# A four-layer graph network on one core: norm roots, ReLU, block kinds and planner costs of the first stage, and new planner costs elsewhere

## The chip, the cores and the metric

The kernel runs on one core of a Trainium2 chip, as one launch. Its time is the device time in microseconds of one execution. "Before" is the kernel as it stands, and the profile shown is of one execution of it.

A core has five engines that work at once, each through its own queue in strict order: TensorE (PE in the profile; its weight loads are PEld), VectorE (DVE), ScalarE (ACT), GpSimd (POOL), and SyncE (SP), which here only issues DMAs.

## The reference, cut to what matters

There are 128 graphs of 128 nodes with 128 channels: `x` is [128, 128, 128] in fp32, `adj` is [128, 128, 128] of 0 and 1. Four layers follow each other; each normalises its input, takes the ReLU, and adds its result to `x`.

```python
h = jnp.maximum(_layernorm(x, axis=-1), 0.0)
x = x + _L0_gnn_ref(h, adj, ...)     # layers 1, 2, 3: attention of other kinds
```

The first layer is what the first stage of the kernel works for:

```python
D = jnp.abs(x[:, :, None, :] - x[:, None, :, :])     # |h_i - h_j| of all pairs of nodes
h = jnp.einsum('bijc,oc->bijo', D, W1) + b1          # 64 outputs
m = jnp.mean(h, axis=(0, 1, 2))
v = jnp.mean((h - m) ** 2, axis=(0, 1, 2))
h = (h - m) / jnp.sqrt(v + EPS) * g1 + be1
```

The mean and variance run over all graphs and all pairs, so they have to be known before any pair's score can be used. The rest of the first layer (scores on the edges, softmax, a product with the nodes, a second batch norm over all graphs), and then layers 1 to 3, need them.

## The kernel before

Three stages follow each other.

`statistics()` computes only the mean and variance of the pair values. It works on groups of 4 graphs (`GB`), 32 groups in all. `nodes(g)` loads a group's `x`, normalises it (mean and variance on VectorE; the root, `(var + eps) ** -0.5`, by an add and a pow on GpSimd; subtraction and multiplication on GpSimd), transposes it on TensorE into PSUM (`pt`), and lets ScalarE take the ReLU twice: into SBUF (`he`) and in place in PSUM (`pt`). It also splits the 64 products of each node into three bf16 parts (`us`). `block(b, q)` then treats 32 rows of one graph against 64 (or 63) later nodes each; 4 blocks cover half of all pairs, which is enough because the difference is symmetric. A block is:

- a difference of `he` with its own nodes, 128 x 2048 or 2016 values, on VectorE (all `q == 0`, and 3 or 4 of the 4 blocks `q == 1` of a group) or on GpSimd (the rest, 8 or 9 of 16),
- the absolute value on ScalarE, in place,
- 4 products with `w1T` on TensorE, two of them side by side in the array, into `ph` (3 buffers of two PSUM banks),
- the statistics of `ph`: by two `bn_stats` on VectorE, or by a Square with accumulated sums on ScalarE (the blocks in `by_act`).

Some blocks `q == 0` (the set `larger`) use |a - b| = 2 max(a, b) - a - b: VectorE takes the maximum instead of the difference, ScalarE does nothing, and TensorE adds 12 bf16 products of `both` with the three parts of `us`.

`edge_attention()` computes the first layer's scores, attention and second batch norm. `layers_01()` does what is left for groups of 4 graphs, with up to 8 groups under way.

In every stage the steps are Python generators. Before each step a generator says `yield engine, cost, takes, frees`: the engine, the microseconds that the step is assumed to keep it, and the buffers that it takes and gives back. `in_order` simulates the engines with these costs, always lets the step begin that can begin first, and emits the instructions in that order; `AFTER` adds 0.2 us (2.2 us for a DMA) from the end of a step until its result counts as usable. So the costs set the order of every engine's queue, and with it that of the loads and stores on SP's queue, but nothing else: on the chip each instruction waits for its data.

```python
free_at[engine] = now + work
end = now + work + AFTER[engine]
```

Of the kernel before, what the change touches and what calls it, by code (L numbers as in the profile page):

```python
# [14 lines left out]
AF = mybir.ActivationFunctionType  # L15
ALU = mybir.AluOpType
# [10 lines left out]
GB = 4  # L27
# [29 lines left out]
PE, ACT, DVE, POOL, DMA = "PE", "ACT", "DVE", "POOL", "DMA"  # L57
# [115 lines left out]
def kernel(ctx: ExitStack, tc: tile.TileContext, x, adj, w, out):  # L173
# [316 lines left out]
    def statistics():  # L490

        with tc.tile_pool(name="a2", bufs=2) as a2, tc.tile_pool(
# [6 lines left out]
            larger = {(i, 0) for i in range(3)}  # L501
            by_act = {(i, 3) for i in range(GB)} | {(1, 2), (3, 2)}
# [17 lines left out]
            def nodes(g):  # L520
# [5 lines left out]
                yield DVE, 1.3, "", ""  # L526
# [6 lines left out]
                yield POOL, 3.3, "xn", "xg"  # L533
                rs = a2.tile([P, GB], F32, tag="ln_rs", name="ln_rs")
                nc.gpsimd.tensor_tensor(rs, mv[:, :, 1], eps, ALU.add)
                nc.gpsimd.tensor_tensor(rs, rs, nhalf, ALU.pow)
# [4 lines left out]
                yield PE, 0.45, "pt", "xn"  # L541
# [3 lines left out]
                yield ACT, 1.0, "he", ""  # L545
# [3 lines left out]
                nc.scalar.activation(pt, pt, AF.Relu)  # L549
# [4 lines left out]
                yield PE, 0.8, "ph us", ""  # L554
# [4 lines left out]
                yield ACT, 0.31, "", ""  # L559
                nc.scalar.copy(us[:, 0], pu)  # L560
                yield DVE, 0.36, "", ""
                nc.vector.tensor_tensor(pu, pu, us[:, 0], ALU.subtract)
                yield ACT, 0.31, "", ""
                nc.scalar.copy(us[:, 1], pu)
                yield DVE, 0.34, "", "ph"
# [4 lines left out]
            def pairs(b):  # L570
# [10 lines left out]
                if not left[g]:  # L581
                    yield "free", "he pt us"
                    yield DVE, 0.5, "", "six"
                    nc.vector.bn_aggr(st[:, g, :], six.pop(g).rearrange("p a b -> p (a b)"))

            def block(b, q):
# [7 lines left out]
                is_larger, on_act = (i, q) in larger, (i, q) in by_act  # L594
                by_dve = q == 0 or (q == 1 and (i < 3 or g % 2))
                yield "after", ("six", g)
                yield (DVE, 2.26, "d", "") if by_dve else (POOL, 3.58, "d", "")
# [5 lines left out]
                if by_dve:  # L603
                    own = bcast(hp[:, i0 : i0 + QR], 2, w_)
                    nc.vector.tensor_tensor(dv, later, own, ALU.max if is_larger else ALU.subtract)  # L605
# [4 lines left out]
                if not is_larger:  # L610
                    yield ACT, 2.1 if on_act else 1.92, "", ""
# [4 lines left out]
                yield PE, 3.15 if is_larger else 1.73, "ph", "d"  # L616
# [16 lines left out]
                if on_act:  # L633
                    yield ACT, 1.25, "", "ph"
# [3 lines left out]
                else:  # L638
                    yield DVE, 1.42, "", "ph"
# [60 lines left out]
    def edge_attention():  # L700
# [3 lines left out]
        with tc.tile_pool(name="b2", bufs=2) as b2p, tc.tile_pool(name="b3", bufs=B_W) as b3p, tc.tile_pool(  # L704
# [80 lines left out]
            def group(g):  # L785
# [12 lines left out]
                yield POOL, 0.85, "", ""  # L798
# [7 lines left out]
                yield POOL, 1.9, "", ""  # L806
# [3 lines left out]
                yield PE, 0.85, "p p", ""  # L810
# [5 lines left out]
                yield DVE, 0.8, "", "p"  # L816
# [7 lines left out]
                yield DVE, 1.9, "", "p"  # L824
# [6 lines left out]
                yield PE, 0.4, "p", ""  # L831
# [30 lines left out]
            def parts(g, xn, made):  # L862
                yield ACT, 0.6, "", ""
                h1 = tile_h("h1")
                nc.scalar.activation(h1, xn, AF.Relu)
                yield DVE, 0.62, "", ""
# [4 lines left out]
                yield POOL, 1.8, "", ""  # L871
# [5 lines left out]
            def values(g, ht, made):  # L877
                yield PE, 1.0, "p", ""
# [3 lines left out]
                yield ACT, 0.6, "", "p"  # L882
# [3 lines left out]
            def check(g, adjb):  # L886

                yield PE, 0.6, "p", ""
# [6 lines left out]
                yield ACT, 0.75, "", "p"  # L895
# [7 lines left out]
            def bases(g, adjb, made):  # L903
                yield ACT, 0.6, "", ""
                base = tile_f("base")
                nc.scalar.activation(base, adjb, AF.Identity, bias=far, scale=-NEG)
                yield POOL, 1.9, "", ""
# [5 lines left out]
            def graph(g, i, inc, made):  # L913
# [3 lines left out]
                yield PE, 0.95, "q", ""  # L917
# [8 lines left out]
                yield ACT, 0.75, "d", "q"  # L926
                d = b2p.tile([P, 2, SLOT_N // 2], F32, tag="d", name="d", bufs=3)
                nc.scalar.activation(d, diff[:, :, 0 : SLOT_N // 2], AF.Abs)  # L928
                yield PE, 0.6, "p", "d"
# [3 lines left out]
                yield ACT, 0.5, "", "p"  # L933
                z = made["z"][:, i, :]
                nc.scalar.activation(z, ph, AF.Identity, bias=h_bi, scale=h_sc)  # L935
                yield DVE, 0.48, "", ""
                leaky(nc.vector, z, z, 0.01)
                yield PE, 0.5, "p", ""
# [11 lines left out]
                yield DVE, 0.13, "", "p"  # L950
# [10 lines left out]
                yield ACT, 0.75, "it", ""  # L961
                it = b2p.tile([P, 5, P], F32, tag="it", name="it", bufs=3)
                nc.scalar.copy(it, pi)  # L963
                yield DVE, 0.75, "", "p"
# [4 lines left out]
                yield PE, 1.25, "" if i else "p", "it"  # L969
# [8 lines left out]
            def attention(g, made):  # L978
                yield DVE, 1.45, "", "p"
# [6 lines left out]
                yield ACT, 2.1, "", ""  # L986
# [7 lines left out]
                yield DVE, 0.8, "", ""  # L994
# [3 lines left out]
                yield PE, 0.5, "p", ""  # L998
# [3 lines left out]
                yield ACT, 0.6, "eT", "p"  # L1002
                eT = tile_f("eT", 2)
                nc.scalar.copy(eT, pt)
                yield PE, 1.0, "p", ""
# [9 lines left out]
                yield DVE, 1.5, "", "w yt"  # L1015
# [501 lines left out]
    def layers_01(first_in):  # L1517

        with tc.tile_pool(name="c_in", bufs=3) as c_in, tc.tile_pool(
# [31 lines left out]
            def normal(x, out):  # L1551

                yield DVE, 1.75, "", ""
# [6 lines left out]
                yield ACT, 0.45, "", ""  # L1560
# [3 lines left out]
                yield POOL, 2.5, "t", ""  # L1564
# [5 lines left out]
            def transposed(xn, out, frees):  # L1570
                yield PE, 1.1, "ps", frees
# [3 lines left out]
                yield ACT, 0.62, "t", "ps"  # L1575
# [8 lines left out]
            def single_head(z, own, mask, least, values, ones_at, after, out):  # L1584

                yield ACT, 1.6 if own else 0.7, "t", "ps"
# [8 lines left out]
                yield DVE, 0.72, "", ""  # L1595
                masked_larger(t.rearrange(flat), mask.rearrange(flat), least)
                yield "join",
                yield PE, 1.1, "pz", "t v"
                po = weighted(t, values, ones_at + 1)
                yield DVE, 0.9, "t", "pz"  # L1600
                xh = over_sums(po, ones_at)
                yield "fork", positive(xh, after, out)
                yield ACT, 0.65, "t", ""
# [3 lines left out]
                yield DVE, 0.7, "", "t t t"  # L1607
# [5 lines left out]
            def positive(xh, after, out):  # L1613
                yield DVE, 0.62, "t", ""
# [34 lines left out]
            def with_bias3(x3):  # L1649
                yield POOL, 0.95, "", ""  # L1650
                nc.gpsimd.tensor_tensor(x3, x3, bcast(pb_bc, 1, GC), ALU.add)

            def head_attention(i, f1d, fl, mask, es, ps_):
                yield PE, 0.45, "pz w", ""
# [7 lines left out]
                yield ACT, 1.27, "", ""  # L1662
# [5 lines left out]
                yield DVE, 1.27, "", "pz"  # L1668
# [3 lines left out]
            def two_graphs(k, f1d, fl, mask, h1T, es, xT):  # L1672
# [4 lines left out]
                yield PE, 1.0, "ps vals", ""  # L1677
# [3 lines left out]
                yield DVE, 0.7, "", "ps"  # L1681
# [5 lines left out]
                yield PE, 2.6, "ps ps", "w w vals"  # L1687
# [18 lines left out]
                yield ACT, 1.25, "t", "ps"  # L1706
# [4 lines left out]
                yield DVE, 0.69, "", "ps t"  # L1711
# [4 lines left out]
            def type_scores(t, h3T, dstT, by_type):  # L1716
                yield PE, 0.63, "ps", ""
                pp = psum("pp")
                nc.tensor.matmul(pp, aq[:, t, :], h3T, start=True, stop=True)  # L1719
                yield ACT, 0.6, "t", "ps"  # L1720
# [4 lines left out]
            def with_h1(xn, x1, res):  # L1725
                yield DVE, 0.69, "t", "t t"
# [701 lines left out]
```

## Time and profile before

| what | value |
|---|---|
| median of 3 runs | 2766.36 us (2764.8 to 2766.55) |
| the profiled execution | 2765.68 us, span 2763.8 us |
| mean granted TensorE clock | 0.970 |
| busy share of the span | PE 92%, DVE 86%, ACT 78%, POOL 61% |
| first stage | 28 to about 1133 us |
| second stage | about 1133 to 1830 us |
| third stage | about 1830 to 2764 us |

The busy shares of the whole span mix three stages with different limits. They have to be read stretch by stretch: which engine is full, and who waits for whom. A row of a group of instructions names the line, the engine, the operation and its tiles, then the count, the busy time, the mean duration of one, and how long the engine had stood idle before such instructions and what ended that.

### The profile page before, as it was taken

To read this page: it belongs to the slowest core of one execution; us is meant where nothing else is said; L and a number is where in the kernel's file an instruction comes from. 1 tells how busy PE (TensorE), PEld (TensorE's weight loads), DVE (VectorE), ACT (ScalarE), POOL (GpSimd) and SP (SyncE) were. 2 spreads that over 40 slices of the span, in tenths; PEclk is the share of its full clock that TensorE was granted. 3 is DMA by queue.
4 is the path that set the end of the run, shared out by engine and by line. 5 is a ranking of instruction groups with operands and counts; after the bars stand their busy time and mean duration, and the time that the engine had idled before them with its cause. 6 is when DMAs were issued, how large, how long until landed. Compare 5 with 4: busy or idle time off the path is not lost. (4 is left out here: it accounts for less than half of the span.)

```text
span 2763.8 us, 52563 instructions
## 1 busy us (share of the span) xinstructions
PE 2529.2 (92%) x19981; PEld 1568.7 (57%) x19981; DVE 2376.3 (86%) x4596; ACT 2148.8 (78%) x3563; POOL 1675.7 (61%) x1007
## 2 busy tenths in 40 slices
PE   6999999999999999799999999967989988988887
PEld 2334343343434343377777777756767766777665
DVE  6999999899999998778888888859889887888986
ACT  4999999999999999656666666548788887788885
POOL 7999999999999999644443434112333333333225
PEclk8999999999999999899999999979999999999999
DMA  2000000000000000322222222030111110111001
GB/s 67 17 31 24 24 24 24 24 24 24 23 24 24 24 20 12 121 82 89 79 92 75 83 83 77 19 126 21 44 36 45 47 57 28 45 43 32 9 5 29
DMA packets 134261, 122.67 MB, mean 44 GB/s; under 512 B 9504, under 2 KB 100960, under 8 KB 134000
## 3 DMA queue, kind: packets, MB, share of 16 engines
q1 hardware_dynamic: 131360, 117.83, 13.8%
q8 instruction: 161, 2.64, 0.4%
q10 hardware_dynamic: 2032, 1.31, 0.2%
q14 instruction: 100, 0.82, 0.1%
q0 software_dynamic: 608, 0.07, 0.0%
HBM read 73.05 MB, written 46.14 MB: 43 GB/s over the span
## 5 line engine op out<-in xcount | busy, mean ns | idle before, releaser
L608 POOL TENSOR_TENSOR d<-he 128x2016 f32<-128x2016 f32 (+1 forms) x272 | 959.5, 3561 | 12.1 <-PE ph L629 12.1
L629 PE MATMUL ph<-d,w1T 128*64 128x512 f32 (+1 forms) x4096 | 911.3, 594 | 23.4 <-ACT d L612 16.2
L612 ACT ACTIVATE d<-d 128x2016 f32<-128x2016 f32 (+1 forms) x416 | 772.6, 1885 | 5.2 <-POOL d L608 4.1
L629 PEld LDWEIGHTS ph<-d,w1T 128*64 128x64 f32 x4096 | 314.9, 136 | 538.5 <-issue 454.5
L605 DVE TENSOR_TENSOR d<-he,pt 128x2048 f32<-128x2048 f32 x240 | 542.2, 2274 | 6.9 <-PE ph L629 6.2
L641 DVE BATCH_NORM_STATS2 six<-ph 128x6 f32<-128x512 f32 (+1 forms) x640 | 405.0, 681 | 64.9 <-PE ph L629 63.9
L1566 POOL TENSOR_TENSOR xn<-xo,mv 128x512 f32<-128x512 f32 x64 | 77.7, 1214 | 311.6 <-DVE mv L1559 222.0
L635 ACT ACTIVATE ph<-ph 128x1008 f32<-128x1008 f32 x192 | 191.5, 998 | 51.2 <-PE ph L629 35.3
L973 PE MATMUL pl<-its,it 128*128 128x128 f32 x1280 | 171.6, 283 | 7.0 <-DVE its L966 6.7
L873 POOL CAST h<-xn 128x512 bf16<-128x512 f32 x32 | 20.0, 626 | 253.7 <-DVE xn L867 201.1
L973 PEld LDWEIGHTS pl<-its,it 128*128 128x128 f32 x1280 | 157.0, 195 | 21.7 <-DVE its L966 13.4
L1669 DVE SCALAR_TENSOR_TENSOR p<-z,mask 128x1024 f32<-128x1024 f32 x124 | 148.5, 1212 | 11.7 <-ACT z L1667 11.6
L1567 POOL TENSOR_TENSOR xn<-xn,rs 128x512 f32<-128x512 f32 x96 | 108.1, 1126 | 67.1 <-ACT rs L1563 55.9
L629 PE MATMUL ph<-both,us 128*64 128x512 bf16 x1152 | 142.3, 380 | 0.0
L935 ACT ACTIVATE z<-ph,h_bi,h_sc 128x320 f32<-128x320 f32 x128 | 78.4, 619 | 77.2 <-PE ph L932 76.6
L1667 ACT ACTIVATE z<-z 128x1024 f32<-128x1024 f32 x128 | 129.0, 1008 | 4.1
L921 PE MATMUL diff<-inc,h 128*128 128x320 bf16 x768 | 129.2, 305 | 0.7 <-ACT d L928 0.5
L841 DVE SCALAR_TENSOR_TENSOR inc<-in_row,row 128x12 bf16<-128x12 f32 (+12 forms) x512 | 125.7, 314 | 3.7 <-PE in_row L834 3.6
L928 ACT ACTIVATE d<-diff 128x640 f32<-128x640 f32 x128 | 89.9, 702 | 49.1 <-PE diff L921 48.6
L963 ACT CAST it<-pi 128x640 f32<-128x640 bf16 x128 | 86.6, 689 | 50.7 <-PE pi L960 50.2
L629 PEld LDWEIGHTS <-us 128*64 128x64 bf16 x1152 | 73.4, 111 | 90.7 <-issue 56.9
L1914 POOL TENSOR_TENSOR xh<-xh,xo 128x512 f32<-128x512 f32 x32 | 45.5, 1422 | 124.7 <-DVE xh L1635 108.7
(350 smaller groups left out, 5422.4 us busy)
## 6 DMA issues: line engine op xcount, KB each, us to landing
ht<-h SPq DMA_DIRECT2D x64, 256.0 KB, 2.8
xg<-in_x SPq DMA_DIRECT2D x32, 256.0 KB, 2.8
n<-ln_xn SPq DMA_DIRECT2D x32, 256.0 KB, 2.4
h<-he SPq DMA_DIRECT2D x32, 256.0 KB, 2.6
adj<-in_adj SPq DMA_DIRECT2D x32, 256.0 KB, 3.2
xn<-n SPq DMA_DIRECT2D x32, 256.0 KB, 2.7
xb<-in_x SPq DMA_DIRECT2D x32, 256.0 KB, 3.2
xb<-xb SPq DMA_DIRECT2D x32, 256.0 KB, 2.0
```

The costliest lines, as they stand in the source:

```text
L605: nc.vector.tensor_tensor(dv, later, own, ALU.max if is_larger else ALU.subtract)
L608: nc.gpsimd.tensor_tensor(dv, later, own, ALU.subtract)
L612: nc.scalar.activation(d[:, 0 : 4 * n], d[:, 0 : 4 * n], AF.Abs, accum_out=sums[:, g, k : k + 1] if on_act else None,)
L629: nc.tensor.matmul(ph[64 * a : 64 * a + 64, t, 0:n], wt, x_, start=part == 0, stop=not is_larger or part == 3,)
L635: nc.scalar.activation(ph[:, :, 0:n], ph[:, :, 0:n], AF.Square, accum_out=squares[:, g, k : k + 1])
L641: nc.vector.bn_stats(six[g][:, 2 * by_bn.index((i, q)) + t, :], ph[:, t, 0:n])
L841: nc.vector.scalar_tensor_tensor(inc[:, :, e : e + n], in_row[:, :, 0:n], float(k + 1), row[:, :, 0:n], ALU.is_equal, ALU.subtract,)
L921: nc.tensor.matmul(diff[:, a, 0 : SLOT_N // 2], h[:, i, :], inc[:, a * SLOT_N // 2 : (a + 1) * SLOT_N // 2], start=m == 0, stop=m == 2,)
L973: nc.tensor.matmul(made["pl"][:, i, :], it[:, k, :], its[:, k, :], start=k == 0, stop=k == 4)
L1567: nc.gpsimd.tensor_tensor(xn, xn, bcast(rs, 2, P), ALU.mult)
L1667: nc.scalar.activation(z, z, AF.Exp, scale=1.0 - SLOPE)
L1669: nc.vector.scalar_tensor_tensor(p, z, 1.0, bcast(mask[:, i, :], 1, NH), ALU.max, ALU.mult)
```

## The change

In the first stage:

- The roots of the norm go from GpSimd (add and pow) to ScalarE (Ln, then Exp with scale -0.5, on 128 x 4 values). The activation table that has both is loaded at the head of the stage.
- ScalarE no longer writes the ReLU back into `pt`. VectorE's differences read the unrectified `pt` and rectify it on the way: `tensor_tensor(later, own)` becomes `scalar_tensor_tensor(max(own, 0), later)`.
- Two blocks of a group use the maximum (`i < 2`) where three did.
- One block of a group, (3, 2), has its statistics on VectorE instead of ScalarE: 11 and 5 where 10 and 6 were.

In all three stages the costs in the `yield` lines are replaced. Outside `statistics()` nothing else changes.

```diff
@@ -491,6 +491,7 @@
+        nc.scalar.preload_act_table_set("natural_log_exp_and_others")
         with tc.tile_pool(name="a2", bufs=2) as a2, tc.tile_pool(
             name="a_d", bufs=A_D
         ) as a_d, tc.tile_pool(name="a_ph", bufs=3, space=PSUM) as a_ph, tc.tile_pool(
@@ -498,8 +499,7 @@
         ) as a_ps:
             n_parts = NB // GB
             blocks = [(i, q) for i in range(GB) for q in range(NQ)]
-            larger = {(i, 0) for i in range(3)}
-            by_act = {(i, 3) for i in range(GB)} | {(1, 2), (3, 2)}
+            by_act = {(i, 3) for i in range(GB)} | {(1, 2)}
             by_bn = [k for k in blocks if k not in by_act]
             ACT_N, BN_N = (
                 sum(QR * width[q] for _, q in some) for some in (sorted(by_act), by_bn)
@@ -523,46 +523,46 @@
                 yield DMA, 0.6, "xg", ""
                 xg = a2.tile([P, GB, P], F32, tag="xg", name="xg")
                 nc.sync.dma_start(xg, x_t[:, b0 : b0 + GB, :])
-                yield DVE, 1.3, "", ""
+                yield DVE, 1.6, "", ""
                 s6 = a2.tile([P, GB, 6], F32, tag="ln_s6", name="ln_s6")
                 mv = a2.tile([P, GB, 2], F32, tag="ln_mv", name="ln_mv")
                 for i in range(GB):
                     nc.vector.bn_stats(s6[:, i, :], xg[:, i, :])
                     nc.vector.bn_aggr(mv[:, i, :], s6[:, i, :])
-                yield POOL, 3.3, "xn", "xg"
+                yield ACT, 0.35, "", ""
                 rs = a2.tile([P, GB], F32, tag="ln_rs", name="ln_rs")
-                nc.gpsimd.tensor_tensor(rs, mv[:, :, 1], eps, ALU.add)
-                nc.gpsimd.tensor_tensor(rs, rs, nhalf, ALU.pow)
+                nc.scalar.activation(rs, mv[:, :, 1], AF.Ln, bias=eps_c)
+                nc.scalar.activation(rs, rs, AF.Exp, scale=-0.5)
+                yield POOL, 2.1, "xn", "xg"
                 xn = a2.tile([P, GB, P], F32, tag="ln_xn", name="ln_xn")
                 nc.gpsimd.tensor_tensor(xn, xg, bcast(mv[:, :, 0], 2, P), ALU.subtract)
                 nc.gpsimd.tensor_tensor(xn, xn, bcast(rs, 2, P), ALU.mult)
                 nc.sync.dma_start(xn_d[g], xn)
-                yield PE, 0.45, "pt", "xn"
+                yield PE, 0.56, "pt", "xn"
                 pt = a_ps.tile([P, GB, P], F32, tag="pt", name="pt")
                 for i in range(GB):
                     nc.tensor.transpose(pt[:, i, :], xn[:, i, :], ident)
-                yield ACT, 1.0, "he", ""
+                yield ACT, 0.5, "he", ""
                 he = a2.tile([P, GB, W], F32, tag="he", name="he")
                 nc.scalar.activation(he[:, :, 0:P], pt, AF.Relu)
                 nc.sync.dma_start(h_d[g], he[:, :, 0:P])
-                nc.scalar.activation(pt, pt, AF.Relu)
                 yield POOL, 0.42, "", ""
                 nc.gpsimd.tensor_copy(he[:, :, P:W], he[:, :, 0 : W - P])
-                yield PE, 0.8, "ph us", ""
+                yield PE, 1.03, "ph us", ""
                 pu = a_ph.tile([P, GB, 64], F32, tag="ph", name="pu")
                 for i in range(GB):
                     nc.tensor.matmul(pu[:, i, :], he[:, i, 0:P], w1T, start=True, stop=True)
                 us = a2.tile([P, 3, GB, 64], BF16, tag="us", name="us")
-                yield ACT, 0.31, "", ""
+                yield ACT, 0.28, "", ""
                 nc.scalar.copy(us[:, 0], pu)
-                yield DVE, 0.36, "", ""
+                yield DVE, 0.33, "", ""
                 nc.vector.tensor_tensor(pu, pu, us[:, 0], ALU.subtract)
-                yield ACT, 0.31, "", ""
+                yield ACT, 0.28, "", ""
                 nc.scalar.copy(us[:, 1], pu)
-                yield DVE, 0.34, "", "ph"
+                yield DVE, 0.33, "", "ph"
                 nc.vector.tensor_tensor(us[:, 2], pu, us[:, 1], ALU.subtract)
                 ready[g] = he, pt, us
                 yield "done", ("nodes", g)
@@ -580,7 +580,7 @@
                 left[g] -= 1
                 if not left[g]:
                     yield "free", "he pt us"
-                    yield DVE, 0.5, "", "six"
+                    yield DVE, 0.6, "", "six"
                     nc.vector.bn_aggr(st[:, g, :], six.pop(g).rearrange("p a b -> p (a b)"))
             def block(b, q):
@@ -591,10 +591,10 @@
                 g, i = b // GB, b % GB
                 w_, i0, n = width[q], QR * q, 8 * width[q]
-                is_larger, on_act = (i, q) in larger, (i, q) in by_act
+                is_larger, on_act = q == 0 and i < 2, (i, q) in by_act
                 by_dve = q == 0 or (q == 1 and (i < 3 or g % 2))
                 yield "after", ("six", g)
-                yield (DVE, 2.26, "d", "") if by_dve else (POOL, 3.58, "d", "")
+                yield (DVE, 2.18 if q == 0 else 2.15, "d", "") if by_dve else (POOL, 3.53, "d", "")
                 he, pt, us = ready[g]
                 hb, hp, us = he[:, i, :], pt[:, i, :], us[:, :, i, :]
                 d = a_d.tile([P, QR * 64], F32, tag="d", name="d")
@@ -602,18 +602,20 @@
                 later = shifted(hb[:, i0 + 1 : i0 + 1 + w_], QR)
                 if by_dve:
                     own = bcast(hp[:, i0 : i0 + QR], 2, w_)
-                    nc.vector.tensor_tensor(dv, later, own, ALU.max if is_larger else ALU.subtract)
+                    nc.vector.scalar_tensor_tensor(
+                        dv, own, 0.0, later, ALU.max, ALU.max if is_larger else ALU.subtract
+                    )
                 else:
                     own = bcast(hb[:, i0 : i0 + QR], 2, w_)
                     nc.gpsimd.tensor_tensor(dv, later, own, ALU.subtract)
                 k = sorted(by_act).index((i, q)) if on_act else None
                 if not is_larger:
-                    yield ACT, 2.1 if on_act else 1.92, "", ""
+                    yield ACT, 1.88 if on_act else 1.81, "", ""
                     nc.scalar.activation(
                         d[:, 0 : 4 * n], d[:, 0 : 4 * n], AF.Abs,
                         accum_out=sums[:, g, k : k + 1] if on_act else None,
                     )
-                yield PE, 3.15 if is_larger else 1.73, "ph", "d"
+                yield PE, 3.17 if is_larger else 1.76, "ph", "d"
                 ph = a_ph.tile([P, 2, 512], F32, tag="ph", name="ph")
                 every4 = "p (r x j) -> p x r j"
                 by_part = d[:, 0 : 4 * n].rearrange(every4, x=4, j=w_)
@@ -631,12 +633,12 @@
                                 start=part == 0, stop=not is_larger or part == 3,
                             )
                 if on_act:
-                    yield ACT, 1.25, "", "ph"
+                    yield ACT, 1.03, "", "ph"
                     nc.scalar.activation(
                         ph[:, :, 0:n], ph[:, :, 0:n], AF.Square, accum_out=squares[:, g, k : k + 1]
                     )
                 else:
-                    yield DVE, 1.42, "", "ph"
+                    yield DVE, 1.22, "", "ph"
                     for t in range(2):
                         nc.vector.bn_stats(six[g][:, 2 * by_bn.index((i, q)) + t, :], ph[:, t, 0:n])
```

In `edge_attention()` and `layers_01()` only costs change; some of them:

```diff
...
-                yield POOL, 0.85, "", ""
+                yield POOL, 0.68, "", ""
                 adjb = tile_h("adjb", B_IN)
...
-                yield DVE, 1.45, "", "p"
+                yield DVE, 2.0, "", "p"
                 base, pl = made["base"], made["pl"]
...
             def normal(x, out):
-                yield DVE, 1.75, "", ""
+                yield DVE, 1.1, "", ""
...
-                yield POOL, 2.5, "t", ""
+                yield POOL, 2.1, "t", ""
                 xn = tile_t("xn")
...
-                yield ACT, 1.27, "", ""
+                yield ACT, 1.13, "", ""
                 z = z.rearrange("p s (h j) -> p (s h) j", h=HH)
...
-                yield PE, 2.6, "ps ps", "w w vals"
+                yield PE, 2.05, "ps ps", "w w vals"
...
             def scaled(ph2, h2):
-                yield ACT, 1.6, "", "pz"
+                yield ACT, 0.95, "", "pz"
...
```

## The prediction

> **What bounds the kernel now.** I read the page's slices first, then cut the span into stretches and asked for each engine's busy time in each, then the groups of instructions by shape, and last the waits and the timeline of the first stage. A measurement of this kernel can tell about 0.2%, or 5.5 us, from no change.
>
> The stretches (columns: stretch, length, busy us of PE, PEld, DVE, ACT and POOL with instruction counts, then granted clock, DMA share, GB/s):
>
> ```profile
> 60.00:460.00 400.00, 396.62 (x2098) 161.39 (x2096) 376.62 (x461) 374.79 (x413) 398.27 (x159) 1.00 0.07 23
> 460.00:1060.00 600.00, 584.42 (x3072) 235.73 (x3070) 548.80 (x668) 556.03 (x613) 587.50 (x239) 1.00 0.08 24
> 1116.00:1133.00 17.00, 17.00 (x88) 6.10 (x84) 12.05 (x15) 15.15 (x17) 0.39 (x1) 1.00 0.01 1
> 1180.00:1740.00 560.00, 535.24 (x4666) 414.19 (x4665) 476.00 (x1213) 345.93 (x734) 239.17 (x218) 0.98 0.26 81
> 1900.00:2640.00 740.00, 657.56 (x7405) 518.12 (x7404) 640.28 (x1466) 597.50 (x1304) 245.96 (x231) 0.97 0.13 37
> ```
>
> The first stage (about 28 to 1133 us) keeps GpSimd and TensorE full: POOL is busy 99.6% of the early stretch and 97.9% of the late one, PE 99.2% and 97.4%, while DVE and ACT have 6 to 9% to spare. The middle stage (to about 1830) has PE at 96%. In the last stage PE has 89%, DVE 87%, ACT 81%: no engine is full, and the order of issue decides. The DMA share is at most 0.26 in these stretches: no transfer bounds them.
>
> The groups that matter (count, busy us, mean ns, then idle time before and its releaser):
>
> ```profile
> L608 POOL TENSOR_TENSOR d<-he 128x2016 f32<-128x2016 f32 x256 | 902.6, 3558 | 12.1 <-PE ph L629 12.1
> L605 DVE TENSOR_TENSOR d<-he,pt 128x2048 f32<-128x2048 f32 x240 | 542.2, 2274 | 6.9 <-PE ph L629 6.2
> L629 PE MATMUL ph<-both,us 128*64 128x512 bf16 x1152 | 142.3, 380 | 0.0
> L612 ACT ACTIVATE d<-d 128x2048 f32<-128x2048 f32 x160 | 301.1, 1902 | 1.1 <-DVE d L605 1.1
> L641 DVE BATCH_NORM_STATS2 six<-ph 128x6 f32<-128x512 f32 x512 | 325.7, 682 | 49.8 <-PE ph L629 48.8
> L536 POOL TENSOR_TENSOR ln_rs<-ln_rs,nhalf 128x4 f32<-128x4 f32 x32 | 32.3, 1010 | 2.5
> L1562 ACT ACTIVATE rs<-mv,eps_c 128x4 f32<-128x4 f32 x96 | 28.0, 292 | 13.8 <-DVE mv L1559 13.5
> L1563 ACT ACTIVATE rs<-rs 128x4 f32<-128x4 f32 x96 | 19.7, 206 | 3.0
> L549 ACT ACTIVATE pt<-pt 128x512 f32<-128x512 f32 x32 | 19.0, 592 | 0.0
> L1616 DVE SCALAR_TENSOR_TENSOR xo<-xh,x1h 128x512 f32<-128x512 f32 x32 | 25.6, 800 | 0.4
> L1908 DVE TENSOR_TENSOR p<-p,q 128x512 f32<-128x512 f32 x32 | 24.8, 775 | 14.5 <-ACT q L1906 12.3 <-issue 2.1
> L1669 DVE SCALAR_TENSOR_TENSOR p<-z,mask 128x1024 f32<-128x1024 f32 x124 | 148.5, 1212 | 11.7 <-ACT z L1667 11.6
> ```
>
> POOL waits in its differences 12.1 us only, and for PE: the two fill each other. Spacings are shorter than durations, because an instruction starts before the one ahead has left. I take them from the timeline, start to start: POOL difference 3.515 (7 in 24.7 us), DVE difference 2.195, a pair of bn_stats 1.21, ACT Abs 1.80 (1.87 with its accumulator read), Square with its read 1.02, one PE block 1.72 and its 12 bf16 matmuls 1.30 more (60.51 to 61.81).
>
> **Load of the first stage per group of 4 graphs, before** (32 groups, 16 blocks each). POOL: 8.5 x 3.515 + roots 1.26 + two norm steps 2.12 + copy 0.36 = 33.6. PE: 584.4 busy us at a pace of 34.4 (POOL's 33.6 over its 97.9%) is 33.5. DVE: 7.5 x 2.195 + 10 x 1.21 + node work 2.3 + aggregate 0.6 = 31.4. ACT: 7 x 1.80 + 6 x 1.87 + 6 x 1.02 + two ReLU 1.0 + two casts 0.58 = 31.5. POOL ran from 28.1 to 1116.4: 1088.3 us, a pace of 34.0, 1.2% over the largest load. Then PE drained its backlog alone to 1132.9.
>
> **The change part by part.**
>
> *Roots to ScalarE.* POOL loses the add and the pow, which take 1.26 from start to start (881.30 to 882.56): 33.6 - 1.26 = 32.4. ACT gains Ln and Exp, 0.47 in the spacing of the last stage's rows L1562 and L1563. No transfer moves: the store of xn still follows POOL's multiply on SP's queue, and POOL's queue issues no DMA here. The new wait is ACT's, on DVE's statistics; behind it stand the Abs of blocks that PE wants, and POOL's multiply waits for ACT in turn. In the last stage the same chain held POOL 55.9 us over 28 of 96 passes. At that rate 32 passes could cost 18.6 us; at the other end nothing, since the node chain runs a group ahead (POOL waited for DVE's statistics once, at the start). I take 3 us, inside the allowance below.
>
> *ReLU into the differences.* ACT loses `pt<-pt`, 0.5 in spacing. The DVE difference becomes a scalar_tensor_tensor of the same 2048 columns. Its row is not there. L1669 reads PSUM with the same operation: 1024 columns in 1.212 us, which is 0.145 over one column per 0.96 GHz cycle; L605 has 0.141 over. So 2.28 against 2.274: nothing (ends -0.03 and +0.03 each). The Trainium skill, *Vector Engine (DVE) Microarchitecture Reference*, section "Points that are easy to get wrong", speaks against this: a scalar_tensor_tensor with two non-bf16 SBUF sources runs at half throughput. L1616 has two fp32 SBUF sources and takes 800 ns, where the tensor_tensor L1908 takes 775: no halving here, and in the first stage one source lies in PSUM. By the rule DVE would need 16 more us a group and the total some 3260; the rows decide, I count nothing.
>
> *Two larger blocks for three.* PE loses 12 bf16 matmuls a group: 33.5 - 1.3 = 32.2. ACT gains one Abs, 1.80.
>
> *Block (3,2) from Square to bn_stats.* ACT loses 1.02 and 0.07; DVE gains 1.21.
>
> *The table.* One more table load (1.28 us, as L1526's) falls where ACT sits idle 11.7 us for the first transfer. The Trainium skill, *ScalarE: Activation LUTs*, sections "Table sets" and "What ACT_TABLE_LOAD costs", puts Ln and Exp in one set and counts Abs, ReLU and Copy in all, and prices a switch at 2.66 us. The trace shows one load before all Ln, Exp and ReLU of the last stage, but no Abs or Square after it. With no switch: 0.
>
> Sum per group: POOL 32.4; PE 32.2; DVE 31.4 + 1.2 = 32.6; ACT 31.5 + 0.47 - 0.5 + 1.80 - 1.09 = 32.2. Four engines within 1.3%. Before, two engines together cost 1.2% over the larger load; with four, and only three PSUM buffers for the blocks, I double it: 32.6 x 1.025 = 33.4. Gain (34.0 - 33.4) x 32 = 19 us, the tail after POOL taken as before. Ends: 1.2% gives 32 us, 4.3% gives nothing.
>
> *New planner costs.* They change no operation, only the order on the four engines, and with it SP's order of loads and stores. Adding one group's costs in `layers_01`: PE 28.3 becomes 25.9, where the trace has 805.6 busy us from 1835 to the end, 25.2 a group. DVE goes from 27.2 to 24.4, ACT 25.0 to 22.4, POOL 9.9 to 9.1. All shrink by 8 to 11%, so most of the order should survive; what shifts is short chains (`normal` on DVE 1.75 to 1.1, where the timeline has 1.06). What can be won is idle PE: 82 us in the stretch 1900 to 2640, 25 us in 1180 to 1740. I take a tenth of it, 10 us. Bounds: 50 us if the last stage came to the middle one's 4.4% idle, and a loss of as much as the slower rival's below.
>
> Sum: 19 + 10 = 29. The profiled execution took 2765.7 us (span 2763.8 and 1.9 around it), 0.7 below the median of 2766.4, so I make no correction: **2736 us**.
>
> **The rivals.**
>
> *The likeliest (0.56):* as above, 2736, its own range 2718 to 2752.
>
> *The order gains more (0.16).* For it: the last stage's idle time is spread over short waits of many kinds (the largest for PE, 13.2 us below). Against: costs shrank nearly in proportion. Half of its 82 us with 19 from the first stage: 2706.
>
> ```profile
> PE po L1626 <- DVE p L1669: 13.2, 8, 3.3
> PE pf L1784 <- ACT hTc L1577: 7.8, 5, 2.7
> ```
>
> *The balance eats the gain (0.14).* Four engines near 98% wait for each other through three PSUM buffers; Ln behind a late DVE stops ACT's Abs. For it: POOL fell from 99.6 to 97.9% with only two full. Pace 33.8 gives 6 us, and with 5 from the order 2755.
>
> *The new order is worse, and the total slower (0.10).* The costs are now spacings, and the planner adds only 0.2 us to the end of each step; where a result lands later than that, an instruction stands at the head of a strict queue too early. Place: the last stage's PE queue. At PE's share 84.5% instead of 88.9% the 658 busy us take 778: +38, net 2785. It decides once that stage loses over 19 + 5.5 us, a share below 86.0%. Against: the old costs were merely larger.
>
> *It doesn't do what it says (0.04).* If Square or Abs were outside the set, two switches a group are 64 x 2.66 = 170 us of ACT, 37.5 a group against 34.0: some 2870.
>
> **How the numbers follow.** Faster by over 0.2% (below 2760.8): 0.56 and 0.16 whole, 0.11 of the third: 0.83. Within 0.2%: 0.03 of the third, 0.03 of the fourth's mild part: 0.06. Slower: the rest of the fourth and the last, 0.11. The range goes from 2706 to 2760 and leaves out about 2 in 10: the fourth and fifth cases, and the lower half of the second.
>
> **What would show it.** POOL's rows L535 and L536 gone, 64 small ACT rows of 0.29 and 0.21 us; DVE differences near 2.28 us x240; 768 bf16 matmuls for 1152; 448 Abs, 160 Squares and 704 block bn_stats; all four engines 96 to 98% busy in the middle of the first stage, which ends near 1114. A difference row near 4.4 us, more than three table loads, or a first stage that ends after 1130 proves me wrong there; a last stage whose PE share moves by over 4 points, in the planner's part.

## The result and the profile after

The changed kernel takes 2715.9 us (median of 6 runs, 2711.5 to 2722.2) against 2766.6 before: a ratio of 0.9816, 95% interval 0.98 to 0.9831, so 50.7 us less. A second measurement, beside the last experiments, gave 2710.6 us and 0.9791 (0.9777 to 0.9805). The prediction was 2736 with a range of 2706 to 2760: the sign and the order of size were right, the gain was forecast at 29 us and is 51 to 57. The first stage was to end near 1114 and ends at 1094.

Where the time went is read from two marks that both profiles have: the first GpSimd pow on 128 x 1 values (`af_rs`, at the end of the first stage) and the cast to `types` (at the end of the middle stage).

| profiled execution | end of first stage | middle stage | last stage | span |
|---|---|---|---|---|
| before | 1138.3 | 692.6 | 932.9 | 2763.8 |
| after | 1094.4 (-43.9) | 677.9 (-14.7) | 939.4 (+6.5) | 2711.7 |

The marks, before and then after (duration in ns, first and last start in us; of `af_rs` the first counts):

```profile
L427 POOL TENSOR_TENSOR af_rs<-af_ve,nhalf x2: 549/552/555, 1138.3 to 1829.6; 128x1 f32<-128x1 f32 x2
L1073 DVE CAST types<-odd x1: 142/142/142, 1830.9 to 1830.9; 1x1 int32<-1x1 f32 x1
```

```profile
L427 POOL TENSOR_TENSOR af_rs<-af_ve,nhalf x2: 557/560/562, 1094.4 to 1771.0; 128x1 f32<-128x1 f32 x2
L1075 DVE CAST types<-odd x1: 142/142/142, 1772.3 to 1772.3; 1x1 int32<-1x1 f32 x1
```

So the first stage brought more than the 19 us of the forecast, the middle stage alone more than the 10 us set down for both later stages, and the last stage lost.

The groups of instructions of the first stage after the change (count, busy us, mean ns, idle before and its releasers):

```profile
L610 POOL TENSOR_TENSOR d<-he 128x2016 f32<-128x2016 f32 x256 | 903.5, 3557 | 15.0 <-DVE six L643 7.8 <-PE ph L631 6.6 <-ACT d L614 0.5
L605 DVE SCALAR_TENSOR_TENSOR d<-pt,he 128x2048 f32<-128x2048 f32 x240 | 541.4, 2269 | 0.7 <-PE ph L631 0.7
L631 PE MATMUL ph<-both,us 128*64 128x512 bf16 x768 | 95.6, 382 | 0.0
L643 DVE BATCH_NORM_STATS2 six<-ph 128x6 f32<-128x512 f32 x512 | 319.5, 678 | 12.6 <-PE ph L631 11.3
L535 ACT ACTIVATE ln_rs<-ln_mv,eps_c 128x4 f32<-128x4 f32 x32 | 9.3, 291 | 7.5 <-DVE ln_mv L531 7.5
L536 ACT ACTIVATE ln_rs<-ln_rs 128x4 f32<-128x4 f32 x32 | 6.6, 206 | 1.0
```

Every operation is there in the forecast number and at the forecast duration. The difference with the ReLU inside takes 2269 ns where the plain one took 2274: the halving that the prediction weighed is not there. The roots on ScalarE take 291 and 206 ns. `bn_stats` before waited 48.8 us for PE's blocks, now 11.3.

The stretches (columns as in the prediction):

```profile
60.00:460.00 400.00, 391.44 (x1991) 157.36 (x1987) 396.16 (x492) 394.67 (x417) 392.00 (x139) 1.00 0.08 23
460.00:1060.00 600.00, 588.87 (x2990) 236.23 (x2988) 592.41 (x734) 588.49 (x617) 590.41 (x211) 1.00 0.08 24
```

In 460 to 1060 PE, DVE, ACT and POOL are busy 98.1, 98.7, 98.1 and 98.4%: all four are full at once, where before only PE and POOL were. ScalarE's table loads are two, as before:

```profile
L494 ACT ACT_TABLE_LOAD x1 | 1.3, 1283 | 6.9 <-DMA a2b<-in_L_gnn_a 6.9
L1528 ACT ACT_TABLE_LOAD x1 | 1.3, 1283 | 5.3 <-DVE types L1075 5.3
```

The load that the change places took the place of the first one (L336 before) instead of joining it, and Abs, Square, Ln, Exp, ReLU and copies ran under it for the whole first stage without another.

### The profile page after: what moved, and what is told of

Read it like the earlier page. It is cut to its first block, busy times and chain, and to the rows that moved or that the text cites. A ratio compares the mean times of both kernels' runs of the same rounds, so it can differ in the third digit from the quotient of the medians.

```text
span 2711.7 us, 51703 instructions
## 1 busy us (share of the span) xinstructions
PE 2497.3 (92%) x19597; PEld 1559.2 (57%) x19597; DVE 2416.1 (89%) x4660; ACT 2161.6 (80%) x3531; POOL 1644.8 (61%) x943
## 5 line engine op out<-in xcount | busy, mean ns | idle before, releaser
L631 PE MATMUL ph<-d,w1T 128*64 128x504 f32 (+1 forms) x4096 | 910.0, 594 | 22.9 <-DVE six L643 13.2
L614 ACT ACTIVATE d<-d 128x2048 f32<-128x2048 f32 (+1 forms) x448 | 832.2, 1888 | 18.1 <-POOL d L610 12.4
L605 DVE SCALAR_TENSOR_TENSOR d<-pt,he 128x2048 f32<-128x2048 f32 x240 | 541.4, 2269 | 0.7 <-PE ph L631 0.7
L643 DVE BATCH_NORM_STATS2 six<-ph 128x6 f32<-128x512 f32 (+1 forms) x704 | 435.8, 676 | 13.4 <-PE ph L631 12.0
L637 ACT ACTIVATE ph<-ph 128x1008 f32<-128x1008 f32 x160 | 159.7, 998 | 9.8 <-PE ph L631 8.8
L1669 ACT ACTIVATE z<-z 128x1024 f32<-128x1024 f32 x128 | 129.0, 1008 | 4.0
L843 DVE SCALAR_TENSOR_TENSOR inc<-in_row,row 128x4 bf16<-128x4 f32 (+12 forms) x512 | 125.5, 315 | 1.2 <-PE in_row L836 1.2
L1568 POOL TENSOR_TENSOR xn<-x,mv 128x512 f32<-128x512 f32 x32 | 36.5, 1139 | 138.3 <-DVE mv L1561 65.9
L968 DVE TENSOR_TENSOR its<-pi,s 128x640 f32<-128x640 bf16 x128 | 102.9, 810 | 15.0 <-ACT it L965 14.1
L1700 PE MATMUL va<-p,vals 128*32 128x128 f32 x2048 | 107.8, 283 | 8.0 <-DVE vals L1685 7.8
```

Of the source, the lines that this page charges most:

```text
L605: nc.vector.scalar_tensor_tensor(dv, own, 0.0, later, ALU.max, ALU.max if is_larger else ALU.subtract)
L614: nc.scalar.activation(d[:, 0 : 4 * n], d[:, 0 : 4 * n], AF.Abs, accum_out=sums[:, g, k : k + 1] if on_act else None,)
L631: nc.tensor.matmul(ph[64 * a : 64 * a + 64, t, 0:n], wt, x_, start=part == 0, stop=not is_larger or part == 3,)
L637: nc.scalar.activation(ph[:, :, 0:n], ph[:, :, 0:n], AF.Square, accum_out=squares[:, g, k : k + 1])
L643: nc.vector.bn_stats(six[g][:, 2 * by_bn.index((i, q)) + t, :], ph[:, t, 0:n])
L843: nc.vector.scalar_tensor_tensor(inc[:, :, e : e + n], in_row[:, :, 0:n], float(k + 1), row[:, :, 0:n], ALU.is_equal, ALU.subtract,)
```

## The experiments

The prediction credited the first stage's gain to the loads, and gave the new costs some idle time of the later stages. Theory 1 kept that: the largest load per group, plus a little, sets the pace. Theory 2: the order that the costs make decides how much of a load's fall is seen.

### Operations and costs of the first stage, apart

First run: the new operations with the old costs; both later stages as before. The costs are taken back from the changed kernel's:

```diff
...
-                yield (DVE, 2.18 if q == 0 else 2.15, "d", "") if by_dve else (POOL, 3.53, "d", "")
+                yield (DVE, 2.26, "d", "") if by_dve else (POOL, 3.58, "d", "")
-                    yield ACT, 1.88 if on_act else 1.81, "", ""
+                    yield ACT, 2.1 if on_act else 1.92, "", ""
-                    yield ACT, 1.03, "", "ph"
+                    yield ACT, 1.25, "", "ph"
-                    yield DVE, 1.22, "", "ph"
+                    yield DVE, 1.42, "", "ph"
...
```

> The first stage's new operations with the old costs in every yield line (the two new steps get old-style costs: ACT 0.45, POOL 2.1); the two later stages as before. Theory 1, the loads: POOL 33.6 to 32.4 and PE 33.5 to 32.2 us a group bring the gain, whatever the costs, so the first stage shortens by 38 to 44 us and the total is near 2725. Theory 2, the order: with old costs that take ACT for the fullest engine, four equally loaded engines wait for each other as I had allowed for (2.5% over the largest load), so the stage shortens by about 19 us and the total is near 2747.

Measured: 2773.1 us, ratio 1.0018 (1.001 to 1.0026). The operations alone make the kernel slightly slower. Both theories were wrong: one expected 40 us, the other 19.

Its stretches and waits between 60 and 1060 us (who waited for whom: us, times, longest):

```profile
460.00:1060.00 600.00, 571.72 (x2882) 213.09 (x2880) 572.72 (x714) 566.99 (x599) 568.74 (x202) 1.00 0.07 23
```

```profile
PE ph L631 <- ACT d L614: 45.3, 44, 1.8
```

```profile
POOL d L610 <- PE ph L631: 25.4, 23, 2.5
```

```profile
ACT ph L637 <- PE ph L631: 38.7, 36, 1.5
```

All four engines are busy only 94.5 to 95.5%. PE waits for ACT's absolute values, ACT's Squares wait for PE, POOL waits for PE to give buffers back. They wait in a ring: no engine is full, and the loads fell for nothing.

Second run: the old operations with the new costs (3.36 for POOL's norm step with the roots in it, 1.0 for ScalarE's two ReLU).

> The old operations of the first stage with the new costs there (POOL's norm step 3.36, ScalarE's two ReLU 1.0); the later stages as before. Theory 1: POOL's load of 33.6 still bounds, at most the 12 us of its waits and some of the 16.5 us of PE's tail can go: total 2755 to 2766. Theory 2: the same ceiling, but most of it taken, about 20 us: near 2747.

Measured: 2752.2 us, ratio 0.9948 (0.9933 to 0.9964); the first stage ends at 1122.4. POOL is busy 99.5% of 460 to 1060, and its differences' wait for PE between 60 and 1060 us shrank from 9.7 us in the kernel before to 1.5:

```profile
460.00:1060.00 600.00, 596.28 (x3140) 240.49 (x3137) 559.08 (x683) 564.00 (x625) 597.18 (x243) 1.00 0.08 24
```

```profile
POOL d L608 <- PE ph L629: 9.7, 8, 1.3
```

```profile
POOL d L608 <- PE ph L629: 1.5, 3, 1.1
```

Here the load of POOL is the ceiling, and the new order reaches it. The time lies between the two theories (2755 or more, and 2747) and decides for neither.

Third run: operations and costs of the first stage, the old costs in both later ones.

> The first stage as after, operations and costs; both later stages with the old costs. Both theories: the first stage shortens by the 44 us that the two profiles show (1138.3 to 1094.4 at the end of its statistics), nothing else moves, total near 2723. If stages are not independent (the clock, transfers), the total differs from that by more than 5 us.

Measured: 2724.8 us, ratio 0.9845 (0.983 to 0.986); the first stage ends at 1094.9 and the later ones take 696.5 and 931.7 us. No stage moved another beyond the spread that the profiles show anyway (see the end). The four ends of the first stage:

| end of the first stage, us | old costs | new costs |
|---|---|---|
| old operations | 1138.3 | 1122.4 |
| new operations | 1140.9 | 1094.9 |

The operations are worth -2.6 us with the old costs and 27.5 with the new; the costs 15.9 with the old operations and 46.0 with the new. The operations have no worth of their own, the costs have some, and both together bring 30 us more than the two single worths added up. Each field of the table is one plan; other plans with the same sums were not tried.

### What was wrong with the old costs

Under the old costs the planner saw, per group of the new operations, ACT at 9 x 1.92 + 5 x 2.1 + 5 x 1.25 + 1.57 = 35.6 us, DVE at 35.1, POOL at 33.0 and PE at 31.8; under the new ones 32.3, 32.5, 32.5 and 32.6.

Eighth run, every cost of the first stage times 1.1 (new first and middle stage, old last one):

> The version of the fourth run, but every cost of the first stage times 1.1. No operation differs. If it is the ratios of the costs between the engines that made the old costs bad: within 4 us of 2703. If it is their absolute size (the old ones were too large on ACT and DVE by some 10%): most of the 46 us between runs 1 and 3 comes back, 2735 or more.

Measured: 2710.2 us, ratio 0.9787 (0.9771 to 0.9803). The first stage ends at 1095.0, the unscaled version's at 1095.3 and 1096.2; the rest of the difference lies in the middle stage, where nothing was changed (682.9 us in this profile, see the end). The factor also left the order of the first stage as it was: by line and shape, the instructions of PE, VectorE and GpSimd follow each other as in the fourth run, and one of ScalarE's stands elsewhere. So the common size of the costs is not it; what is left is the ratios.

Ninth run, the first one with three of its costs put right (Abs, Square, the pair of `bn_stats`):

```diff
-                    yield ACT, 2.1 if on_act else 1.92, "", ""
+                    yield ACT, 1.88 if on_act else 1.81, "", ""
-                    yield ACT, 1.25, "", "ph"
+                    yield ACT, 1.03, "", "ph"
-                    yield DVE, 1.42, "", "ph"
+                    yield DVE, 1.22, "", "ph"
```

> The kernel of the first run (new operations of the first stage, old costs, 2773 us) with three costs put right there: Abs 1.81 and 1.88 for 1.92 and 2.1, Square 1.03 for 1.25, the pair of bn_stats 1.22 for 1.42. These are what made the planner take ACT (35.6 us a group) and DVE (35.1) for much fuller than POOL (33.0) and PE (31.8). If the wrong ratio between the engines was the fault: most of the 48 us between runs 1 and 3 come back, near 2728. If it was the many small costs of the norm steps: above 2755.

Measured: 2739.3 us, ratio 0.9891 (0.9875 to 0.9908). The first stage ends at 1106.4: 34.5 of the 46.0 us between the first and the third run come back with three numbers. The total lies between the two expectations (2728 and above 2755), and the rest must lie in the small costs (node steps, the two differences, PE's blocks); they were not told apart.

### Undoing one operation each, with fitting costs

Base: new first and middle stage, old last stage (2702.8 and 2705.9 us in two measurements, first stage to 1095.3 and 1096.2).

Roots back on GpSimd (fifth run):

```diff
-                yield ACT, 0.35, "", ""
+                yield POOL, 3.36, "xn", "xg"
                 rs = a2.tile([P, GB], F32, tag="ln_rs", name="ln_rs")
-                nc.scalar.activation(rs, mv[:, :, 1], AF.Ln, bias=eps_c)
-                nc.scalar.activation(rs, rs, AF.Exp, scale=-0.5)
-                yield POOL, 2.1, "xn", "xg"
+                nc.gpsimd.tensor_tensor(rs, mv[:, :, 1], eps, ALU.add)
+                nc.gpsimd.tensor_tensor(rs, rs, nhalf, ALU.pow)
```

> The version of the fourth run (new first and middle stage, old costs in the last stage; 2702.8 us), but the roots stay on GpSimd (add and pow, cost 3.36 for the whole norm step). Theory 1, with fitting costs the stage runs at 1.2% over its largest load: POOL is back at 33.6 us a group, pace 34.0 instead of 32.9, total 35 us longer, near 2738. Theory 2, the pace follows the mean of the four loads and the order: the mean rises by 0.2 us, total near 2709.

Measured: 2738.7 us, ratio 0.9894 (0.9877 to 0.991). The first stage ends at 1125.1, 29.8 us later, and POOL is the full engine:

```profile
460.00:1060.00 600.00, 576.55 (x2935) 239.27 (x2933) 578.64 (x721) 565.91 (x571) 597.18 (x241) 1.00 0.08 24
```

With fitting costs the largest load does set the pace, as theory 1 says: POOL's 33.6 us at 99.5% busy is 33.8 a group. The total agrees better than the stage does: 35 us were expected there.

Block (3, 2) back on ScalarE (seventh run):

```diff
-            by_act = {(i, 3) for i in range(GB)} | {(1, 2)}
+            by_act = {(i, 3) for i in range(GB)} | {(1, 2), (3, 2)}
```

> The version of the fourth run, but block (3, 2) keeps its statistics on ScalarE, 10 blocks by bn_stats and 6 by Square. Theory 1: ACT 32.2 + 1.1 = 33.3 us a group (DVE 31.4), pace 33.7, total 25 us longer, near 2728. Theory 2: no change of the mean, total near 2703.

Measured: 2728.2 us, ratio 0.9857 (0.9841 to 0.9874). The total agrees better than the reason: the first stage ends at 1109.3, only 14.0 us later. ACT is the full engine, and at 599.43 of 600 us busy it runs at its load of 33.3 us a group, with nothing of the 1.2% that I had added:

```profile
460.00:1060.00 600.00, 582.76 (x2964) 216.80 (x2962) 565.76 (x690) 599.43 (x668) 585.94 (x210) 1.00 0.08 24
```

The other 8 to 11 us lie in the later stages, where nothing differs from the base.

Three blocks by the maximum, as before (sixth run):

```diff
-                is_larger, on_act = q == 0 and i < 2, (i, q) in by_act
+                is_larger, on_act = q == 0 and i < 3, (i, q) in by_act
```

> The version of the fourth run, but three blocks a group use the maximum, as in the kernel before. Theory 1: PE is back at 33.5 us a group (ACT falls to 30.4), pace 33.9, total 32 us longer, near 2735. Theory 2: the mean of the loads falls by 0.1 us, total near 2700.

Measured: 2759.3 us, ratio 0.9968 (0.9956 to 0.9981). The first stage ends at 1147.6: 52.3 us later where PE's load would give 32.

```profile
460.00:1060.00 600.00, 580.60 (x3060) 248.57 (x3058) 566.15 (x701) 531.79 (x575) 562.82 (x202) 1.00 0.08 24
```

```profile
PE ph L631 <- DVE six L643: 19.6, 19, 1.2
PE ph L631 <- ACT ph L637: 9.0, 10, 1.3
```

PE, which should be full here, is at 96.8%, while it waits for DVE and ACT to empty its three PSUM buffers, and they have time to spare. The second run had the same three blocks and PE at 99.4%. So the order costs some 20 us more here, with costs that fit; why this plan is worse was not settled. It also shows that the change needs its two-block balance as much as its new costs. Taken together, the first stage lost 29.8, 14.0 and 52.3 us where theory 1 said 35, 25 and 32: the largest load sets the floor, and the order still decides how far above it the stage runs.

### The later stages

Fourth run, new first and middle stage, the last stage with its old costs:

> As after, but the last stage with its old costs. If the 6.5 us that the last stage lost between the two profiles come from its new order: near 2709, 0.25% faster than after. If they are one profile's chance: near 2716, as after.

Measured: 2702.8 us, ratio 0.977 (0.9756 to 0.9785); 13 us below the first measurement of the changed kernel, where 7 were expected. Against the third run, the middle stage's costs are worth 22 us. Over all profiles the middle stage took 692.6 to 698.9 us with the old costs (5 profiles, mean 695.4) and 671.6 to 682.9 with the new (9 profiles, mean 676.4): 19 us. Some 13 of them are idle time of PE (53.7 to 56.5 us of the stage before, 40.7 to 44.6 now).

The last stage was then measured once more beside its rivals. The changed kernel again (tenth run):

> The changed kernel once more, beside the two that follow, to measure the last stage's new costs against the old ones without a change of chip between. If the new order of the last stage is worse by itself: 6 to 13 us above the next run (the profiles of one execution gave 6.5, the medians of two calls 13). If it was chance: within 3 us of it.

The version with the old costs in the last stage again (eleventh run):

> The kernel of the fourth run once more (new first and middle stage, old costs in the last): 2703 to 2710, the two values that the same first stage with the same later stages gave in runs 4 and 8.

And the changed kernel with a longer landing time in the last stage's plan (twelfth run):

```diff
-def in_order(makers, most, room, kept):
+def in_order(makers, most, room, kept, landing=0.2):
...
-        end = now + work + AFTER[engine]
+        end = now + work + (AFTER[engine] if engine == DMA else landing)
...
                 Z_KEPT, 0.5,
```

> The changed kernel, but in the last stage the planner counts 0.5 us instead of 0.2 from the end of a step to its use. If the new costs there are worse because they let the planner think that results land too early: the loss goes, total within 4 us of the run before. If the loss is only that of another order with the same buffers, there is no reason for it to go: near the changed kernel, or off by up to 10 us either way.

| last stage's plan | median, us | ratio, interval | last stage in the profile |
|---|---|---|---|
| new costs, 0.2 us to land | 2710.6 | 0.9791 (0.9777 to 0.9805) | 939.1 |
| old costs, 0.2 us | 2705.9 | 0.9775 (0.9761 to 0.979) | 934.0 |
| new costs, 0.5 us | 2702.0 | 0.9762 (0.9745 to 0.9779) | 927.6 |

Eleven profiles with the old costs have 929.8 to 935.7 us in the last stage (mean 932.9); the two with the new have 939.4 and 939.1. So the new costs lose 6 us there, and not by chance. The waits of ScalarE from 1850 to 2600 us, first with the old costs (fourth run), then with the new (tenth run), then with the longer landing time (twelfth run), show one wait that grew:

```profile
ACT rs L1564 <- DVE mv L1561: 8.7, 10, 1.8
```

```profile
ACT rs L1564 <- DVE mv L1561: 24.2, 20, 2.8
```

```profile
ACT rs L1564 <- DVE mv L1561: 14.6, 17, 2.2
```

ScalarE's root stood twice as often at the head of its queue before VectorE's statistics were there. The new cost of `normal` is 1.1 us for 1.75; it is the right spacing, but the planner can then put the root up earlier. With 0.5 us to land (in the plan this also delays when a step's buffers count as given back) the wait falls only part of the way, and yet the stage is shorter than with the old costs. So the time does not follow this wait. The whole last stage, with the old costs (eleventh run), the new (tenth) and the longer landing time (twelfth), shows where the difference is:

```profile
1770.00:2704.00 934.00, 809.78 (x8832) 639.37 (x8832) 782.96 (x1793) 721.27 (x1569) 309.97 (x288) 0.95 0.14 41
```

```profile
1769.70:2708.80 939.10, 816.24 (x8832) 645.32 (x8832) 796.88 (x1793) 720.00 (x1569) 315.25 (x288) 0.94 0.14 41
```

```profile
1772.60:2700.20 927.60, 798.63 (x8832) 630.93 (x8832) 800.90 (x1793) 718.47 (x1569) 317.38 (x288) 0.96 0.14 41
```

PE's idle time (the stretch less PE's busy time) is 124.2, 122.9 and 129.0 us: it neither grew with the new costs nor fell with the landing time. What moved is PE's busy time, as the profile models it, for the same 8832 matmuls, 809.8, 816.2 and 798.6 us, and with it the granted clock, 0.95, 0.94 and 0.96. The first profile of the changed kernel has 815.1 us and 0.94 as well, the eleven with the old costs 806.7 to 810.1 us and 0.95 or 0.96. So the loss does not lie in longer waits of PE but in a longer busy time at a lower granted clock. Since only the order differs, the order brings it about; how it does so is open, and so is whether the landing time helps as such, as any other value also makes another order. Among the versions, the last has the lowest median, but its interval overlaps with that of the old costs.

## Why the prediction was right, and where it was not

- **The bound and the loads** were right. POOL and PE filled the first stage before. After, the busy shares of 460 to 1060 at 32.9 us a group are 32.3 for PE, 32.5 for DVE, 32.3 for ACT and 32.4 for POOL, where the prediction had 32.2, 32.6, 32.2 and 32.4.
- **The price of each operation** was right: 2269 ns for the rectifying difference (2.28 us forecast), 291 and 206 ns for the roots, 12 bf16 matmuls a group gone, and no further table load (even the one was a replacement). The pace behind the 2.28, one column per 0.96 GHz cycle, can be read from two rows of the kernel before with one source in PSUM, this one and L605's 2274 ns for 2048 columns: 1594 ns for 1536 columns more, 1.04 ns a column.

```profile
L1712 DVE TENSOR_TENSOR xT<-va,r 128x512 f32<-128x512 f32 x64 | 43.5, 680 | 11.3 <-ACT r L1710 11.3
```

- **"I double it: 32.6 x 1.025 = 33.4"** is the term that was mis-sized. POOL worked from 26.6 to 1079.9 us: 32.9 a group, 1.0% over the largest load instead of 2.5%. That is 16 us more. PE's tail after POOL was 10 us instead of 16.5, and the start 1.5 us earlier: 19 + 16 + 8 = 43, against the 43.9 measured.
- **"They change no operation, only the order"**, with 10 us for both later stages and none for the first, is the step whose reason failed. In the first stage the costs decide whether the balance can be used at all: without them the operations gave nothing (2773.1), and POOL's pace was 34.2 a group (27.6 to 1122.6 us), 5% over the largest load. I had added up the old and new costs of the last stage, and did not do the same sum for the first.
- **"All shrink by 8 to 11%, so most of the order should survive"** was no guide: the last stage, for which it was said, lost 6 us, and the middle one gained 19.
- **The number** was helped by luck. 2716 lies outside the likeliest case's own range (2718 to 2752); the whole range reached further down for the rival in which the order gains more, and that one looked for its gain in the last stage's idle time. PE's idle time there was 126.2 us before and is 124.3 after: the gain came in the other two stages.
- **The slower rival** named the right place and, for that stage, the right sign. Its reason, waits that lower PE's share, is not what the profiles show: PE's share of the last stage was 86.5% before and is 86.8% after. The 6 us, not 38, go with a longer busy time at a lower granted clock.
- **The rival of the eaten balance** (four engines near 98% waiting for each other) did not come true, but the first run comes close to its picture: the same operations under a plan with the wrong ratios, at 94.5 to 95.5%.
- **Two small slips** in the sums: 33.6 over 97.9% is a pace of 34.3, not 34.4, which makes PE's load 33.4, and 2765.7 less 29 is 2737. Neither matters.

## What to carry to other kernels

When a planner's costs set the queues of four engines, add the costs up per engine before judging a change of load: if the sums rank the engines otherwise than the trace does, lowering the real bound may bring nothing. Here the ratios mattered, and a factor of 1.1 on all costs changed next to nothing. Costs taken from start to start in a trace brought 46 us in the first stage (with the new operations) and 19 in the second, and lost 6 in the third: measure a new order stage by stage, and there look at PE's busy time, its idle time and the granted clock apart. Measure operations and costs apart too, in a table of four: here the operations had no worth without the costs, and the costs a third of theirs without the operations.

## What the runs showed of the hardware that I had not expected

Six profiles with the same first stage ended it between 1094.4 and 1096.2 us, but nine profiles with the same middle stage took 671.6 to 682.9 us, with the same plan. The shortest and the longest of these nine (fourth and eighth run):

```profile
1095.30:1766.90 671.60, 630.94 (x5479) 488.28 (x5479) 562.34 (x1492) 408.27 (x864) 284.80 (x259) 0.97 0.26 82
```

```profile
1095.00:1777.90 682.90, 639.93 (x5468) 495.49 (x5479) 566.22 (x1491) 408.60 (x864) 284.72 (x259) 0.95 0.26 81
```

Of the 11.3 us between them, 9.0 are PE's busy time, at a granted clock of 0.95 for 0.97. In order of length, the nine stages have a granted clock of 0.97 four times, then 0.96 four times, then 0.95; the first stage had 0.99 or 1.00 in all six profiles. What lowered the clock in one execution and not in another was not shown. A difference of under 10 us between two single executions of this kernel therefore says little before the stage and its granted clock have been looked at.
